# A depthwise 13x13 convolution by a two-output FIR scheme: three TensorE products in place of four, with the phases of its input stored apart

## The chip, the cores and the metric

The kernel runs on one core of a Trainium2 chip. Its engines work side by side, each through its own instruction queue: TensorE (PE: matmuls, with PEld its weight loads), VectorE (DVE), ScalarE (ACT), GpSimd (POOL) and SyncE (SP, which only issues DMAs). ACT and POOL issue DMAs too. The metric is the device time of one execution in microseconds (us), the median of several runs.

## What is computed

`x` is (T=4, B=8, 512, 512) fp32: 4 x 8 = 32 images of 512 x 512. Four layers follow one another, each a residual on a group norm (four groups, each of two neighbouring `b`, for each `t`):

```python
x = x + layer0(_gn(x), ...)       # spiking attention: lif(linear), q k^T v, linear, lif
x = x + layer1(_gn(x), w)         # depthwise 13x13, the same w for each channel
x = x + layer2(_gn(x), ...)       # 3x3, 8 to 8 channels, 8-bit quantised
x = x + layer3(_gn(x), ...)       # 3x3, 8 to 8 channels
...
def layer1(x, w):
    xp = jnp.pad(x, ((0, 0), (0, 0), (6, 6), (6, 6)), mode='reflect')
    return conv(xp, w, strides=(1, 1), padding='VALID', groups=8)
...
def _gn(v, G=4, eps=1e-5):        # over the two channels of a group and all pixels
    return (v - mean(v)) / sqrt(var(v) + eps)
```

`lif` makes each output of layer 0 a 0 or a 1 (a threshold on a running potential), so layer 0 adds spikes to `x`. Layer 2 quantises by `127 / max|gn(x)|`, so it needs the mean, the variance, the maximum and the minimum of layer 1's output before it can begin.

## The kernel before

**Layer 0** (L260 to L1112) goes over the 32 pairs (b, t) and for each over four tiles of 128 tokens. `unit` (L583 to L677) computes the q, k and v spikes by matmuls; in it GpSimd adds `h += twice` (L655, two adds of 128x512 in a row), whose result VectorE reads at L615. `settle` (L893) finishes the group norm of a later input; it raises to the power -1/2 on GpSimd (L184). `project_out` (L789 to L850) ends a tile: output matmuls (L803), ScalarE copies of the input into the tile `x1` (L819, two), the potential `v` (L825), two VectorE operations that add the spikes (`is_ge`, `add`, L827) with their statistics (L831), the reset of the potential (L833), then on GpSimd eight small copies that fill the reflected edges (L839), and one GpSimd DMA that writes the tile's 128 rows of 2096 bytes to DRAM (L844). There are 128 such tiles. In the tile a row is kept as four phases: column 4u + f of the padded row stands in phase f at place u (131 places).

**Layer 1** (class `Layer1`, L1190 to L1298) then goes over the four groups, in a group over two b, and over four t: 32 images. An image is loaded by two SP DMAs (`load_image`, L1168) into a tile `x` of 112 partitions (28 input rows x 4 phases) with 32 windows of 16 output rows x 131 places. `image_bands` (L1181, VectorE) makes four weight matrices of 112 x 64 (one for each shift z = 0..3 of u), with the norm's scale and the residual in them. The convolution along a row is then four products of shifted views, summed in PSUM; rows and phases are the contraction. In `image`, for each of four chunks of an image, eight matmuls (four z, two halves q, which write PSUM partitions 0 to 63 and 64 to 127) go into a bank `ps_conv1`:

```python
for z in range(SHIFTS):                       # L1220
    for q in range(2):
        ...
        nc.tensor.matmul(ps[q*M1:(q+1)*M1, :], lhsT=bt[:, z, :], rhs=xt[:, w0:w0+N_PS1, z:z+NV], ...)   # L1223
```

ScalarE evicts the bank with the norm's offset (L1230, 128x512), VectorE takes its statistics (L1232) and its maximum and minimum (L1238, two reductions). Eight DMAs store an image (L1245), four issued by ScalarE and four by GpSimd, 128 KB each. `ps_c` has four banks; `x` has three buffers, the output tile `xo` two. `next_norm` (L1270) makes the statistics of a finished group, among them two small matmuls (L165), and is placed after the first image of the next group.

**Layers 2 and 3** (from L1387) are written in an order set by hand and are not touched.

The order of instructions within each engine's queue in layers 0 and 1 is set when the kernel is built, by a planner with costs of its own, under the constraints of data and of `issue_after` (an instruction is placed no earlier than another). It is fixed in the program: on the chip each engine works through its queue in that order.

Of the kernel before, what the change touches and what calls it, by code (L numbers as in the profile page):

```python
# [35 lines left out]
F32 = mybir.dt.float32  # L36
# [25 lines left out]
X1_R, X1_U = N + 2 * R1, (D + 2 * R1) // PH  # L62
SHIFTS = 4
K1_P, M1 = W1_IN * PH, W1_OUT * PH
N_PS1 = 4
# [18 lines left out]
COLS = BN + ["L0_conv_gate_scale", "L0_conv_gate_shift"]  # L84

# [38 lines left out]
def network(ctx: ExitStack, tc: tile.TileContext, i: dict, out: bass.AP):  # L124
# [3 lines left out]
    x1d = [[tc.dram_tile([X1_R, PH * X1_U], F32, name=f"x1_{t}_{b}") for b in range(B)] for t in range(T)]  # L128
# [67 lines left out]
    mr1 = const.tile([P, G, T], F32, name="mr1")  # L196
# [3 lines left out]
    def norm1(g, psum):  # L200

        m, r = group_stats(
            st1[g].rearrange("p t b c k (h z) -> p t (b c k h) z", z=3), T, PAIR * NC * 4, None,
            avg, psum, f"x1_{g}", n_each=D // 4, share=0.5,
        )
        nc.vector.tensor_copy(r1[:, g, :], r)
        nc.vector.tensor_mul(mr1[:, g, :], m, r)
# [5 lines left out]
    with ExitStack() as s:  # L213
        head = layer0(
            s, tc, i, x_in, x1d, ident, block, avg, group_stats, group_steps, st1, norm1, band1d, r1,
            w_sum, shared,
# [18 lines left out]
    with ExitStack() as s:  # L235
        ps_1 = s.enter_context(pool("ps_2", space=PSUM))
        st2 = s.enter_context(pool("st2")).tile(
            [P, T, B, W1_N // 2 // N_PS1, 6], F32, name="st2"
        )
        layer1 = Layer1(  # L240
            s, tc, x1d, x2d, avg, group_steps, r1, mr1, st2, m2, r2, most, w_sum, head, ps_1, pool
# [18 lines left out]
def layer0(  # L260
    s, tc, i, x_in, x1d, ident, block, avg, group_stats, group_steps, st1, norm1, band1d, r1, w_sum, shared
# [28 lines left out]
    share = wpool.tile([3 * SQ, P], BF16, name="share")  # L290
# [61 lines left out]
    def phases(x):  # L352
        return x.rearrange("p (v g) -> p g v", g=PH)
# [97 lines left out]
    def prepare_out():  # L451
# [4 lines left out]
        nc.scalar.copy(scale.rearrange("p (g v) -> p g v", g=PH), phases(along_free(a_rows, 3)))  # L456
        wps = [scratch[:, 1 + k % 2, :] for k in range(NC)]

        def scaled(k):
            nc.scalar.mul(  # L460
                wps[k].rearrange("p (g v) -> p g v", g=PH), phases(wp_rows[k]),
                gate_scale[:, k : k + 1],
            )
# [21 lines left out]
        nc.scalar.copy(c_p.rearrange("p (g v) -> p g v", g=PH), phases(along_free(c_rows, 3)))  # L485
        shift = ps_mm.tile([P, D], F32, tag="mm", name="shift")
        for k in range(NC):
# [5 lines left out]
        nc.vector.tensor_mul(  # L493
            moved.rearrange("p (g v) -> p g v", g=PH), phases(shift),
            scale.rearrange("p (g v) -> p g v", g=PH),
        )
# [86 lines left out]
    def unit(kind, cc, n, got):  # L583
# [81 lines left out]
        if kind == "kv":  # L665
            op = nc.tensor.matmul(
                b, lhsT=share, rhs=c_step, start=False, stop=True, skip_group_check=True
# [121 lines left out]
    def project_out(so, c, xt, b, t):  # L789
# [3 lines left out]
        last = D + 2 * R1 - 1  # L793
# [18 lines left out]
        by_phase = phases(xt)  # L812
        halves = []
        for z in range(2):
            f, u = (2 * z + R1) % PH, (2 * z + R1) // PH
            two = slice(2 * z, 2 * z + 2)
            halves.append((two, x1[:, f : f + 2, u : u + NV]))
            with tc.issue_after(seeds[-1]):
                op = nc.scalar.copy(halves[z][1], by_phase[:, two, :])  # L819
# [6 lines left out]
        for z, (two, own) in enumerate(halves):  # L826
            nc.vector.scalar_tensor_tensor(  # L827
                own, v.rearrange("p (g v) -> p g v", g=PH)[:, two, :], 1.0, own,
                op0=ALU.is_ge, op1=ALU.add,
            )  # L830
# [3 lines left out]
        for f in range(PH):  # L834
            right = D + R1 + (f - R1 - D) % PH
            for first, end, mirror in ((f, R1, 2 * R1), (right, last + 1, 2 * (last - R1))):
                n = len(range(first, end, PH))
                u, fm, um = first // PH, (mirror - first) % PH, (mirror - first) // PH
                nc.gpsimd.tensor_copy(  # L839
                    x1[:, f, u : u + n], x1[:, fm, um - n + 1 : um + 1][:, ::-1]  # L840
                )
# [943 lines left out]
```

## Time and profile before

| what | value |
|---|---|
| median of 3 runs | 2706.03 us (2703.67 to 2710.02) |
| profiled execution | 2708.08 us |
| its span in the profile | 2706.3 us (1.8 us lie around it) |
| mean granted TensorE clock | 0.988 |
| PE busy over the span | 2601.4 us (96%) |
| DVE, ACT, POOL busy | 1938.4 (72%), 1239.0 (46%), 762.1 us (28%) |
| layer 0 | 0 to about 1854 us |
| layer 1, first to last matmul | 1853.6 to 2312.4 us |
| first image of layer 2's input made | 2322.6 us |

The span runs from the first to the last instruction that the profile holds. Each engine's busy time is the union of its instructions' times; a share of busy time says nothing by itself of what sets the end, since an average hides stages with different limits. A line of a group names the source line, engine, operation, output and inputs, shape and count; behind the first bar stand the busy time and the mean of one in ns, behind the second the idle time of the engine just before these instructions and what ended it. "<-issue" there means that the profile shows no semaphore that was waited for: the engine's own queue was occupied. An fp32 matmul appears as two records.

### The profile page before, as it was taken

Reading aid. Unit: us, or ns where it says so; the run is one execution under the profiler, and the core shown is the slowest. Engines: PE = TensorE matmul, PEld = TensorE weight load, DVE = VectorE, ACT = ScalarE, POOL = GpSimd, SP = SyncE. Lnnn points to the kernel's source line nnn. Section 1 sums busy time; section 2 is a strip of 40 time slices with the busy share of each in tenths; the row PEclk is TensorE's granted clock in tenths of the full one; section 3 lists DMA queues with packets and bytes.
Section 4 is the critical chain, followed back from the end, with each engine's and each line's share of the span. In section 5 each row is a group of like instructions: output and inputs, shape, how many; then the busy total and the mean of one; then the engine's idle time right before and its main releaser. Section 6 shows DMA issues by size and latency. Waiting matters only on the chain. (4 is left out here: it accounts for less than half of the span.)

```text
span 2706.3 us, 49605 instructions
## 1 busy us (share of the span) xinstructions
PE 2601.4 (96%) x18124; PEld 1502.4 (56%) x18124; DVE 1938.4 (72%) x4054; ACT 1239.0 (46%) x2093; POOL 762.1 (28%) x2040
## 2 busy tenths in 40 slices
PE   7899999999999999999999999998999999699999
PEld 4566666665666656666566566664333333344446
DVE  7877878779788787977877768756565556666550
ACT  1454554555545545455554554553212112566653
POOL 3322223223232222322312323223111111444440
PEclk9999999999999999999999999999999999889999
DMA  6553533434435344253443442446777778567755
GB/s 143 143 153 103 129 119 101 138 113 116 131 96 146 120 115 131 80 149 119 119 120 82 108 109 80 122 124 159 207 213 211 199 206 223 140 183 215 212 162 152
DMA packets 420664, 385.02 MB, mean 142 GB/s; under 512 B 22675, under 2 KB 339843, under 8 KB 420307
## 3 DMA queue, kind: packets, MB, share of 16 engines
q1 hardware_dynamic: 364659, 307.93, 43.8%
q0 software_dynamic: 16448, 51.27, 5.2%
q10 hardware_dynamic: 39312, 22.65, 3.0%
q8 instruction: 142, 2.33, 0.4%
q14 instruction: 103, 0.84, 0.1%
HBM read 278.09 MB, written 103.67 MB: 141 GB/s over the span
## 5 line engine op out<-in xcount | busy, mean ns | idle before, releaser
L1223 PE MATMUL ps_conv<-x,bt 112*64 112x512 f32 x2048 | 451.5, 596 | 5.2 <-DVE v_p L825 3.0
L839 POOL COPY x1s<-x1s 128x1 f32<-128x1 f32 x1000 | 194.2, 248 | 736.0 <-DVE x1s L827 703.8
L1223 PEld LDWEIGHTS ps_conv<-x,bt 112*64 112x64 f32 x2048 | 148.5, 136 | 297.5 <-issue 290.7
L803 PE MATMUL ps_out<-wp,so 128*128 128x512 f32 x1024 | 298.8, 435 | 5.9 <-ACT ps_out L800 4.1
L1230 ACT ACTIVATE xo<-ps_conv,off 128x512 f32<-128x512 f32 x128 | 87.9, 687 | 376.4 <-PE ps_conv L1223 314.8
L571 PE MATMUL ps_kv_b<-w_sums,x_sum 128*128 128x512 f32 x512 | 247.2, 605 | 10.1 <-DVE x_sum L940 7.7
L571 PE MATMUL ps_kv_a<-w_raw,x_raw 128*128 128x512 f32 x512 | 249.8, 606 | 7.3 <-ACT ps_kv_a L637 6.5
L803 PEld LDWEIGHTS ps_out<-wp,so 128*128 128x128 f32 x1024 | 191.1, 189 | 106.1 <-ACT ps_out L800 38.4
L1663 PE MATMUL ps_conv<-x,band_t 32*32 32x512 f32 x6144 | 231.2, 597 | 1.0 <-ACT o L1703 1.0
L655 POOL TENSOR_TENSOR h_kv<-h_kv,twice 128x512 f32<-128x512 f32 x96 | 126.4, 1339 | 340.3 <-ACT twice L652 339.8
L722 PE MATMUL ps_own<-table_own,v 128*128 128x256 bf16 x1536 | 191.8, 273 | 13.8 <-DMA table_own<-bias_parts 9.8
L722 PEld LDWEIGHTS <-v 128*128 128x128 fp8e4 x1536 | 148.2, 98 | 53.9 <-DMA table_own<-bias_parts 19.0
L1245 POOL DMA_DIRECT2D x<-xo x128 | 71.4, 564 | 343.8 <-ACT xo L1230 335.5
L1558 DVE SCALAR_TENSOR_TENSOR x<-ps_conv,inv,x 128x512 f32<-128x512 f32 x128 | 95.3, 750 | 101.7 <-PE ps_conv L1522 91.6
L758 ACT COPY ps_f<-ps_own 64x512 f32<-64x512 f32 x256 | 142.9, 558 | 37.6 <-issue 20.0
L571 PEld LDWEIGHTS ps_kv_b<-w_sums,x_sum 128*128 128x128 f32 x512 | 97.8, 193 | 112.1 <-issue 91.0
L1663 PEld LDWEIGHTS ps_conv<-x,band_t 32*32 32x32 f32 x6144 | 115.2, 103 | 72.9 <-issue 48.9
L819 ACT COPY x1s<-xr 128x256 f32<-128x256 f32 x250 | 151.9, 660 | 4.6 <-DVE h_p L833 2.3
L571 PEld LDWEIGHTS ps_kv_a<-w_raw,x_raw 128*128 128x128 f32 x512 | 95.1, 192 | 101.6 <-issue 82.6
L1185 DVE SCALAR_TENSOR_TENSOR bt<-band,r,eye 112x64 f32<-112x64 f32 x128 | 31.5, 367 | 166.1 <-PE ps_conv L1223 164.0
L1522 PE MATMUL ps_conv<-xq,band 64*64 64x512 bf16 x1536 | 127.2, 404 | 22.5 <-DVE x L1558 16.4
L799 ACT CAST so<-q 128x512 fp32r<-128x512 fp8e4 x128 | 78.8, 617 | 141.0 <-PE ps_out L803 137.0
(257 smaller groups left out, 5076.3 us busy)
## 6 DMA issues: line engine op xcount, KB each, us to landing
table_own<-bias_parts SPq DMA_DIRECT2D x128, 576.0 KB
x<-x SPq DMA_DIRECT2D x64, 917.0 KB
xq<-in_x SPq DMA_DIRECT2D x128, 256.0 KB
xr<-in_x SPq DMA_DIRECT2D x128, 256.0 KB
x<-x1s POOLq DMA_DIRECT2D x125, 262.0 KB, 2.7
out<-o SPq DMA_DIRECT2D x120, 256.0 KB
xs<-in_x SPq DMA_DIRECT2D x112, 256.0 KB
x<-x SPq DMA_DIRECT2D x128, 224.0 KB
```

Of the source, the lines that this page charges most:

```text
L571: mm = nc.tensor.matmul(ps, lhsT=x[:, kk, cc * P : (cc + 1) * P], rhs=w[:, :2, kk, :], start=start and kk == 0, stop=kk == 1, skip_group_c ...
L655: nc.gpsimd.tensor_add(h, c if t == 0 else h, twice[0])
L722: nc.tensor.matmul(out, lhsT=src[:, c, h].rearrange("p t e -> p (t e)"), rhs=table[:, z, u : u + HN], start=start and c == 0 and z == 0, s ...
L758: nc.scalar.copy(final[j][a][two * DH : (two + 1) * DH, :], rows[a * DH : (a + 1) * DH, :])
L803: nc.tensor.matmul(ps, lhsT=tokens[:, k, :], rhs=wpT[z][:, k, :], start=False, stop=k == NC - 1 and z == 1, skip_group_check=True,)
L819: op = nc.scalar.copy(halves[z][1], by_phase[:, two, :])
L839: nc.gpsimd.tensor_copy(x1[:, f, u : u + n], x1[:, fm, um - n + 1 : um + 1][:, ::-1])
L1223: mm = nc.tensor.matmul(ps[q * M1 : (q + 1) * M1, :], lhsT=bt[:, z, :], rhs=xt[:, w0 : w0 + N_PS1, z : z + NV], start=z == 0, stop=z == SH ...
L1230: nc.scalar.activation(xo[:, a, :], ps, AF.Identity, bias=off[:, t : t + 1])
L1522: mm = nc.tensor.matmul(ps[half, :], lhsT=w["band2"][halves[b], kind, dx, :], rhs=xq[halves[b], j % 2, dx : dx + PH, :], start=dx == 0 and ...
L1558: nc.vector.scalar_tensor_tensor(inner, ps, w["inv"], x, op0=ALU.mult, op1=ALU.add, accum_out=sums[:, 0, :] if summed else None,).ins
L1663: mm = nc.tensor.matmul(ps[c * QP : (c + 1) * QP, :], lhsT=band[g * QP : (g + 1) * QP, int(last), dx, :], rhs=src[:, dx : dx + PH, :], sta ...
```

## The change

Layer 1's sum along a row is done by a two-output scheme. Neighbouring outputs u = 2k and u = 2k + 1 are computed together from the even places E and the odd places O of the row. With the bands B0 to B3:

- shared = (B0 + B1) O[k] + (B2 + B3) O[k+1]
- odd output = shared + B1 (E[k+1] - O[k]) + B3 (E[k+2] - O[k+1])
- even output = shared + B0 (E[k] - O[k]) + B2 (E[k+1] - O[k+1])

That makes six products of 512 columns for two outputs of 512 in place of eight. In detail:

- `project_out` writes each row as eight phases (even u, then odd u, of each of the four); DRAM holds x1 as [row within a window and phase][window x 131]. A tile is written by nine GpSimd DMAs (L877 of the changed kernel) in place of one, its edges are filled by six copies (L874) in place of eight, and the spikes are added by three VectorE operations in place of two. Layout copies of layer 0's constants, done once, are doubled.
- `load_image` takes four SP DMAs with pieces of 4192 bytes in place of two with 524; `image_bands` has a fifth VectorE operation that makes two more matrices.
- `differences` (L1262) makes the tiles `d` (O - E, with the sign taken up in the bands): four subtractions of 112x1040 an image, three on GpSimd and one on VectorE.
- `image` works in two halves j: 4 shared products into a bank `ps_odd` (L1288), a ScalarE copy of it into a bank `ps_even` (L1305), 4 products into each: 12 a half, 24 an image in place of 32. `ps_c` has six banks.
- ScalarE's evictions (L1314) accumulate sums, and a `Square` over 128x1024 (L1320) accumulates the squares; VectorE's statistics of the output go. Maximum and minimum are taken over 1024 elements at once (L1329). `rest` of a half is emitted in the program after the next half's copy.
- Of an image's eight stores, ScalarE issues four and SP four (L1342).
- `next_norm` is placed after the second image of the next group and begins with five small VectorE operations (`gather`, L1382).

The diff, cut to these parts:

```diff
+def x1_rows(dst, row, n):
+
+    w, i = divmod(row, W1_OUT)
+    size = X1_W * X1_U
+    return bass.AP(
+        dst.tensor, dst.offset + i * PH * size + w * X1_U, [[PH * size, n], [size, PH], [1, X1_U]]
+    )
...
-    x1d = [[tc.dram_tile([X1_R, PH * X1_U], F32, name=f"x1_{t}_{b}") for b in range(B)] for t in range(T)]
+    x1d = [[tc.dram_tile([W1_OUT * PH, X1_W * X1_U], F32, name=f"x1_{t}_{b}") for b in range(B)] for t in range(T)]
...
-        halves = []
-        for z in range(2):
-            f, u = (2 * z + R1) % PH, (2 * z + R1) // PH
-            two = slice(2 * z, 2 * z + 2)
-            halves.append((two, x1[:, f : f + 2, u : u + NV]))
...
+        odd = bass.AP(
+            flat.tensor, flat.offset + X1_E + 1,
+            [flat.ap[0], [2 * X1_U - 1, 2], [X1_U, 2], [1, NV // 2]],
+        )
+        halves = [
+            (
+                xt.rearrange("p (k g) -> p g k", g=2 * PH)[:, 2 : 2 + PH],
+                x1[:, :, 1 : 1 + NV // 2],
+            ),
+            (xt.rearrange("p (k q f) -> p q f k", q=PH, f=2)[:, ::-3], odd),
+        ]
+        for x, own in halves:
             with tc.issue_after(seeds[-1]):
-                op = nc.scalar.copy(halves[z][1], by_phase[:, two, :])
+                op = nc.scalar.copy(own, x)
...
-        for z, (two, own) in enumerate(halves):
-            nc.vector.scalar_tensor_tensor(
-                own, v.rearrange("p (g v) -> p g v", g=PH)[:, two, :], 1.0, own,
-                op0=ALU.is_ge, op1=ALU.add,
-            )
+        for z, (_, own) in enumerate(halves):
+            cut = v[:, z * HN : (z + 1) * HN]
+            cut = cut.rearrange("p (f k) -> p f k", f=PH)
+            parts = [(cut, own)] if z == 0 else [(cut[:, 2 * e : 2 * e + 2], own[:, e]) for e in range(2)]
+            for on, to in parts:
+                nc.vector.scalar_tensor_tensor(to, on, 1.0, to, op0=ALU.is_ge, op1=ALU.add)
...
-        nc.gpsimd.dma_start(dst[at : at + P, :], flat)
...
+        for to, of in MIRRORED:
+            nc.gpsimd.tensor_copy(pair(flat, *to), pair(flat, *of))
+        cuts = [0, *range(W1_OUT - R1, P, W1_OUT), P]
+        for first, end in zip(cuts, cuts[1:]):
+            nc.gpsimd.dma_start(x1_rows(dst, R1 + c * P + first, end - first), x1[first:end])
...
-    row, n_half = PH * X1_U, W1_N // 2
-    for w0 in (0, n_half):
-        nc.sync.dma_start(
-            xt[:, w0 : w0 + n_half, :],
-            bass.AP(
-                src.tensor, src.offset + w0 * W1_OUT * row,
-                [[X1_U, K1_P], [W1_OUT * row, n_half], [1, X1_U]],
-            ),
-        )
-
-
-def image_bands(nc, bt, band, b, r, eye):
+    size, n_half = X1_W * X1_U, W1_N // 2
+    for j in range(N_1):
+        for first, end, w in ((0, M1, 0), (M1, K1_P, 1)):
+            nc.sync.dma_start(
+                xt[first:end].rearrange("p (q j w) u -> p j q (w u)", q=2, j=N_1)[:, j],
+                bass.AP(
+                    src.tensor, src.offset + first % M1 * size + (w + j * N_PS1) * X1_U,
+                    [[size, end - first], [n_half * X1_U, 2], [1, N_PS1 * X1_U]],
+                ),
+            )
...
+        scale, op = (nr, ALU.subtract) if z % 2 else (r, ALU.add)
         nc.vector.scalar_tensor_tensor(
-            split[0], band[:, :, b, z, :], r[:K1_P], split[1], op0=ALU.mult, op1=ALU.add
-        )
+            bt[:, z, :].rearrange("p (r o) -> p r o", o=PH), band[:, :, b, z, :], scale[:K1_P],
+            eye[:, z, :].rearrange("p (r o) -> p r o", o=PH), op0=ALU.mult, op1=op,
+        )
+    nc.vector.tensor_sub(bt[:, SHIFTS:, :], bt[:, 0:SHIFTS:2, :], bt[:, 1:SHIFTS:2, :])
...
+        self.dp = s.enter_context(pool("d1", 3))
...
+    def differences(self, xt, b, t):
+
+
+        nc, parts = self.nc, []
+        for j in range(N_1):
+            d = self.dp.tile([K1_P, 2, N_PS1, 2, X1_E - 1], F32, tag="d", name=f"d_{b}_{t}_{j}")
+            for q in range(2):
+                w0 = q * (W1_N // 2) + j * N_PS1
+                own = xt[:, w0 : w0 + N_PS1, :]
+                less = bass.AP(
+                    own.tensor, own.offset + X1_E,
+                    [own.ap[0], [X1_U, N_PS1], [1 - X1_E, 2], [1, X1_E - 1]],
+                )
+                own = bass.AP(
+                    own.tensor, own.offset,
+                    [own.ap[0], [X1_U, N_PS1], [X1_E, 2], [1, X1_E - 1]],
+                )
+                engine = nc.vector if (j, q) == (N_1 - 1, 1) else nc.gpsimd
+                engine.tensor_sub(d[:, q], own, less)
+            parts.append(d)
+        return parts
...
+        def products(ps, bands, src, start):
+
+            for z in range(2):
                 for q in range(2):
-                    w0 = q * n_half + a * N_PS1
                     mm = nc.tensor.matmul(
-                        ps[q * M1 : (q + 1) * M1, :],
-                        lhsT=bt[:, z, :],
-                        rhs=xt[:, w0 : w0 + N_PS1, z : z + NV],
-                        start=z == 0,
-                        stop=z == SHIFTS - 1,
+                        ps[q * M1 : (q + 1) * M1, :], lhsT=bt[:, bands[z], :],
+                        rhs=src(q)[:, :, z : z + n_v],
+                        start=start and z == 0, stop=z == 1, skip_group_check=True,
                     )
-            nc.scalar.activation(xo[:, a, :], ps, AF.Identity, bias=off[:, t : t + 1])
-            at = b % PAIR
-            nc.vector.bn_stats(self.st2[:, t, b, a, :], xo[:, a, :])
-            for end, op in ((hi, ALU.max), (lo, ALU.min)):
-                args = end[:, t, at, a : a + 1], xo[:, a, :], AX.X, op
-                if (b, t, a) == (B - 1, T - 1, n_half // N_PS1 - 1):
-                    self.last_ends.append(args)
-                else:
-                    op = nc.vector.tensor_reduce(*args)
-        if (b, t) == (0, 0):
-            self.started = mm.ins, op.ins
-        dst = self.x2d[t]
+            return mm.ins
+
+        for j in range(N_1):
+            d = parts[j]
+
+            def odd(q):
+                w0 = q * n_half + j * N_PS1
+                return xt[:, w0 : w0 + N_PS1, X1_E:]
+
+            shared = self.ps_c.tile([P, N_PS1 * n_v], F32, tag="conv", name="ps_odd")
+            products(shared, (SHIFTS, SHIFTS + 1), odd, True)
+            even = self.ps_c.tile([P, N_PS1 * n_v], F32, tag="conv", name="ps_even")
+            nc.scalar.copy(even, shared)
+            if self.due:
+                self.due.pop()()
+            self.started_mm = products(shared, (1, 3), lambda q: d[:, q, :, 1], False)
+
+            def rest(j=j, d=d, shared=shared, even=even):
+                products(even, (0, 2), lambda q: d[:, q, :, 0], False)
+                own = xo[:, j * N_PS1 : (j + 1) * N_PS1]
+                for par, ps in ((1, shared), (0, even)):
+                    nc.scalar.activation(
+                        own[:, :, :, par], ps.rearrange("p (w k) -> p w k", w=N_PS1), AF.Identity,
+                        bias=off[:, t : t + 1], accum_out=total[:, t, at, j, par : par + 1],
+                    )
+                flat = own.rearrange("p w k e -> p (w k e)")
+                square = self.op.tile([P, 2 * N_PS1 * n_v], F8, tag="square", name="square1", bufs=1)
+                nc.scalar.activation(
+                    square, flat, AF.Square, bias=self.m1[:, g, t : t + 1], scale=-1.0, saturate=False,
+                    accum_out=squares[:, t, at, j : j + 1],
+                )
+                for end, op in ((hi, ALU.max), (lo, ALU.min)):
+                    args = end[:, t, at, j : j + 1], flat, AX.X, op
+                    if (b, t, j) == (B - 1, T - 1, N_1 - 1):
+                        self.last_ends.append(args)
+                    else:
+                        self.started_op = nc.vector.tensor_reduce(*args).ins
+                if j == N_1 - 1:
+                    self.store(b, t, xo)
+
+            self.due.append(rest)
+        if (b, t) == (B - 1, T - 1):
...
+                engine = nc.sync if f % 2 else nc.scalar
...
+                if g > 0 and b % PAIR == 0 and t == 1:
...
+        def gather():
+            nc.vector.tensor_reduce(
+                mean, total.rearrange("p t b j e -> p t (b j) e"), AX.X, ALU.add
+            )
+            nc.vector.tensor_scalar_mul(mean, mean, 1.0 / n_each)
+            nc.vector.tensor_sub(m2, mean, self.m1[:, g, :].unsqueeze(2).to_broadcast(every))
+            nc.vector.tensor_mul(m2, m2, m2)
+            nc.vector.scalar_tensor_tensor(
+                m2, m2, -1.0 * n_each, squares, op0=ALU.mult, op1=ALU.add
+            )
+
+        gather()
```

## The prediction

> **What bounds the kernel now.** I read the page's engine shares, then busy time by windows, the groups of layer 1 with shapes kept apart, and the waits. Columns of the windows: stretch, length, busy time of PE, PEld, DVE, ACT, POOL, then clock, DMA share, GB/s.
>
> ```profile
> 0.00:1850.00 1850.00, 1787.90 (x7774) 1167.09 (x7775) 1463.47 (x3004) 930.36 (x1616) 512.38 (x1327) 0.99 0.44 118
> 1850.00:1900.00 50.00, 44.84 (x185) 15.26 (x185) 28.41 (x68) 6.75 (x10) 17.19 (x49) 0.93 0.96 223
> 2000.00:2100.00 100.00, 100.00 (x466) 34.02 (x466) 56.72 (x119) 19.94 (x29) 16.66 (x29) 1.00 0.76 209
> ```
>
> Layer 1 (1853.6 to 2312.4) is bound by TensorE alone: busy all 100 us of 100, full clock, DMA at 0.76, VectorE under 0.6, ScalarE at 0.2. Layer 0 is also TensorE's (1788 of 1850), GpSimd there at 28%.
>
> What TensorE's time is made of shows in two windows of 1.70 us (second figure in brackets counts matmul records):
>
> ```profile
> 1869.50:1871.20 1.70, 1.70 (x4) 0.55 (x5) 1.70 (x5) 0.45 (x1) 0.96 (x2) 1.00 1.25 252
> 2010.00:2011.70 1.70, 1.70 (x10) 0.57 (x8) 1.70 (x4) 0.69 (x1) 0.00 (x0) 1.00 1.17 239
> ```
>
> An fp32 matmul is two records. In the steady state the two column halves (q=0, q=1) run side by side: records start in pairs every 0.429 us, so two matmuls take u = 0.858 us. At 1869.5 several matmuls of one half stand in a row, and go one record per 0.43 us: a lone matmul takes a whole u. An image is 32 matmuls, 16 u = 13.73 us, and images do start 13.73 us apart (2006.86, 2020.59, 2034.34).
>
> The groups, and what ScalarE waits for, 1900 to 2300:
>
> ```profile
> L1223 PE MATMUL ps_conv<-x,bt 112*64 112x512 f32 x1816 | 395.7, 592 | 0.0
> L1230 ACT ACTIVATE xo<-ps_conv,off 128x512 f32<-128x512 f32 x114 | 78.4, 687 | 323.8 <-PE ps_conv L1223 285.8 <-issue 33.5 <-DMA x<-xo 4.4
> L1238 DVE TENSOR_REDUCE hi<-xo 128x1 f32<-128x512 f32 x115 | 76.9, 669 | 0.0
> ```
>
> And ScalarE's timeline where an image is stored:
>
> ```profile
> 2047.34 0.69 ACT L1230 ACTIVATE xo<-ps_conv,off 128x512 f32<-128x512 f32 x1 [2.76 <-PE ps_conv L1223]
> 2048.05 3.65 ACTq L1245 DMA_DIRECT2D x<-xo  x4
> 2052.04 0.69 ACT L1230 ACTIVATE xo<-ps_conv,off 128x512 f32<-128x512 f32 x1 [4.02 <-issue]
> ```
>
> Four DMA issues hold ScalarE 3.65 us here (2.77 to 4.41 over the images, 3.45 taken), and the next eviction starts 0.34 us later: "issue", no semaphore. Today four PSUM banks hide this.
>
> **What the Trainium skill says.** "TensorE: Matmul & The Clock Gate", "Part 3: Packing small matmuls": matmuls keep program order in start and end, only weight loads are pulled ahead. The windows above agree: a same-half run isn't overtaken. The same page, "Part 1: The HAM clock gate": the clock is judged in windows of 3413 ns and an idle one is followed by half clock. This trace agrees: clock changes lie on a 3.413 us grid, and each of twelve windows that fell to half clock followed one with TensorE streaming under 0.40 of it. "ScalarE: Activation LUTs", "What ACT_TABLE_LOAD costs": 280 ns + 0.833 ns per element with a pointer operand; 512 elements give 707 ns, the trace has 687. "DMA: Bandwidth & Descriptors", "Issuing engines are not separate DMA queues": moving a DMA to another engine saves sequencer time only; no row here contradicts it.
>
> **The change, part by part, per image.**
>
> *Products.* 24 matmuls for 32: 12 u = 10.30 us if all pair, -3.43. They would pair if issued as the source reads. The static order of the changed kernel's TensorE queue in the steady state differs: four x-products of half 0; then, behind the copy odd to even (`copy0`), odd0-d q0, even0 q0, odd1-x q0, odd0-d q1 and so on, the halves separated; then odd1-d and even1, paired. With strict order the 20 matmuls behind copy0 take 12 u = 10.30 us instead of 10 u. Lower bound 8.58.
>
> *The chain through ScalarE.* Its order is copy0, evict odd0, copy1, evict even0, square 0, evict odd1, evict even1, square 1, four store issues, then copy0 of the next image. TensorE's only work ahead of that copy is the next image's four x-products, 1.72 us. From even1's end to the next copy0's end: semaphore 0.10, evict 0.69, accumulator read and gap 0.09 (the layer 2 squares of 512 elements: 720 with a read of 187, mostly beneath), four issues 3.45 (the square, about 1.15 by the price above, and by layer 2's 1.24 for 1024 elements, lies beneath the first two, as issues were seen beside a running ACTIVATE), 0.12 gap, copy 0.57 (layer 0's PSUM copies: 570), semaphore 0.05: 5.07 us. If issues wait for the square: 6.2. If the four take 2.2 (4 x 0.54, the shortest): 3.8. So the period is 10.30 + 5.07 = 15.37 us against 13.73: +1.64, TensorE idle 3.35 us per image in one piece.
>
> *Clock.* A stall of 3.35 us laid on a 3.413 us grid leaves 2.1 us or more in one window in about three of four positions; the window after runs at half clock and costs about 1.5 us of its 1.7: 0.75 x 1.5 = +1.1. Bounds 0 and 1.7. Period 16.5, +2.75. Times 32: +88 us (no throttle: +52).
>
> *Differences.* Three `tensor_sub` of 1040 elements on GpSimd at 1.274 x 1040/512 = 2.6 us (from L655), 7.8 us; one on VectorE, about 1.4. VectorE loses four bn_stats (4 x 0.685) and reduces 1024 at a time (same elements, 5.2 us), bands +0.5: 7.8 us for 8.0. Neither reaches 13 us: nothing. Without that cover half 0's d-products would wait for GpSimd, up to 5 us.
>
> *Stores, loads.* Four store issues move from GpSimd to SP; queued behind them on SP is the load of the image three ahead, needed over a period later than its landing: nothing. Loads have 4192-byte pieces for 524; DMA doesn't bound layer 1 (0.76 busy while TensorE never waits): nothing.
>
> *Group boundaries, end, seam.* The five gather operations, and the group matmuls that TensorE meets ahead of the next x-products: 4.3 us for 2.0, three times, +7. End of the stage, evict, square and gather before the last norm: +2. Seam: GpSimd has the last five tiles' 45 issues, 25 us, ahead of image 0's differences, so its d-products start near 1871 instead of 1854; part is given back by image 1, which today waits for its load until 1874.13: +8 (0 to +17).
>
> *Layer 0.* Per tile, GpSimd issues nine DMAs for one and does six copies for eight:
>
> ```profile
> L844 POOL DMA_DIRECT2D x<-x1s x124 | 69.5, 561 | 39.4 <-POOL x1s L839 35.9 <-issue 2.9 <-DMA x<-x1s 0.6
> L655 POOL TENSOR_TENSOR h_kv<-h_kv,twice 128x512 f32<-128x512 f32 x96 | 126.4, 1339 | 340.3 <-ACT twice L652 339.8
> ```
>
> 8 x 0.56 - 2 x 0.25 = +4.0 us, 512 us in all; GpSimd goes from 28 to 55%, not the bound. But two of three pairs of the adds L655 start right behind such a DMA. From the first add's start to its reader on VectorE (L615) pass 5.1 to 6.2 us, the pair takes 2.56: 2.5 to 3.6 us of slack for 4.0 of delay, so 0.4 to 1.5, say 0.8, on 53 of the 80 pairs = 42 us late. TensorE has other tiles' work between; I take a third: +15. Bounds 0, and +60 (all of it, and the 16 settle steps by 1 us each). VectorE's third is_ge: 0.14 x 128 = 18 us on an engine at 79%, hidden; ScalarE's layout copies keep their count.
>
> *Sum.* The profiled execution's own time is 2708.1 (span 2706.3 and 1.8 around it): 2708 + 88 + 7 + 2 + 8 + 15 = 2828. It lies 2 above the runs' median of 2706: forecast 2826.
>
> **The rivals.**
> - No throttle, same chain: 2706 + 52 + 32 = 2790. For: a stall split by the few x-products keeps windows above 0.40. Against: windows at half clock in the trace after less idle than this.
> - Shorter chain (issues 2.2 us, period 14.2, or halves that pair after all, 13.7): 2706 + 0 to 15 + 32 = 2738 to 2753.
> - Layer 0 is hit in full: +60 for 15, 2871. For: TensorE there is at 97%, and every late spike step delays something. Against: its slack is of the same size as the delay.
> - Faster: the four issues don't hold copy0. Then even1's end to copy0's end is 5.07 - 3.45 = 1.62 us, less than the 1.72 us of x-products; TensorE never waits, and the period is between 10.3 (all pairs) and 12.0 (14 u): at 10.3, 2706 - 110 + 32 = 2628; at 12.0, 2683. It decides at a period of 13.73 less 1.0 (the +32 elsewhere): copy0 done within 2.4 us of even1's end. For: issues ran beside ACTIVATEs. Against: the timeline's 4.02 <-issue.
>
> **How the numbers follow.** A measurement here can tell 0.2% (5 us) from no change. Chances: forecast 0.38 (2800 to 2850), no throttle 0.20 (2760 to 2800), layer 0 in full 0.15 (2850 to 2890), shorter chain 0.13 (2720 to 2760), faster 0.14 (2620 to 2700, a little of it near no change). Slower 0.84, same 0.03, faster 0.13. Range 2730 to 2885: it leaves out the faster case and some 0.05 at each edge.
>
> **What would show it.** Right: images 15.4 to 16.5 us apart; TensorE busy 73 to 80% of layer 1 with a wait of about 3.3 us per image ended by ScalarE's copy; that copy after "issue"; clock near 0.9 in layer 1; in layer 0 GpSimd at 55% and VectorE waiting for its adds. Wrong: images under 13 us apart, or a copy that starts before the stores.

## The result, and the profile after

| | before | changed |
|---|---|---|
| median | 2706.19 us (4 runs) | 2843.55 us (4 runs, 2837.32 to 2845.87) |
| span of the profiled execution | 2706.3 us | 2840.0 us |
| mean granted clock | 0.988 | 0.962 |
| first matmul of layer 1 starts | 1853.56 | 1851.13 us |
| last eviction of layer 1's first four images starts | 1917.75 | 1968.35 us |
| last eviction of layer 1 starts | 2312.54 | 2436.34 us |
| from there to the end | 393.8 | 403.7 us |

The ratio is 1.0503 (1.0481 to 1.0524): slower by 137 us, forecast 2826, range 2730 to 2885. Each ratio here and below is to runs of the kernel before that were made beside it (medians 2705 to 2710 us).

First the windows of the changed kernel, in the columns of the windows before:

```profile
0.00:1850.00 1850.00, 1785.61 (x7771) 1164.77 (x7772) 1473.27 (x3136) 943.75 (x1620) 954.81 (x2040) 1.00 0.47 118
1875.00:1900.00 25.00, 3.43 (x6) 0.82 (x8) 0.00 (x0) 0.00 (x0) 18.95 (x29) 0.50 0.72 153
2100.00:2200.00 100.00, 79.52 (x284) 30.75 (x282) 60.14 (x83) 39.49 (x82) 43.75 (x19) 0.88 0.80 172
```

Layer 0 takes as long as before although GpSimd is busy 955 us for 512. Then TensorE waits for some 40 us; from 1875 to 1900 VectorE and ScalarE do nothing at all, and GpSimd is busy 19 us. In the second stretch of layer 1 TensorE is busy 80 of 100 us, where it was busy all the time before, at a clock of 0.88.

Some short names: x-products are the matmuls L1288 that read `x`, d-products those that read a tile `d`; odd0, even0, odd1 and even1 are the banks `ps_odd` and `ps_even` of an image's halves 0 and 1, so even1 is what ends an image. ScalarE's timeline there (start, length, instruction, then the idle time before it and what ended it):

```profile
2207.47 0.74 ACT L1314 ACTIVATE xo<-ps_even,off 128x512 f32<-128x512 f32 x1 [0.63 <-PE ps_even L1288]
...
2208.31 1.15 ACT L1320 ACTIVATE square<-xo,m 128x1024 fp8e4<-128x1024 f32 x1
2208.31 1.20 ACTq L1342 DMA_DIRECT2D x<-xo  x2
2209.36 0.19 ACT L1320 ACTIVATION_READ_ACCUMULATOR square<-xo,m 128x1 f32 x1
2209.56 2.10 ACTq L1342 DMA_DIRECT2D x<-xo  x2
2211.69 0.57 ACT L1305 COPY ps_even<-ps_odd 128x512 f32<-128x512 f32 x1 [2.15 <-issue]
```

and TensorE's over the same time:

```profile
2207.70 1.94 PE L1288 MATMUL ps_odd<-x,bt 112*64 112x512 f32 x8 [0.26 <-PE ps_even L1288]
2212.41 1.06 PE L1288 MATMUL ps_odd<-d,bt 112*64 112x512 f32 x2 [2.77 <-ACT ps_even L1305]
```

This is the chain of the prediction: the last eviction, the square with two issues beneath it, two issues alone, the copy; TensorE has its eight records of x-products (four matmuls) and then waits 2.77 us for the copy. Over the 22 images away from group boundaries the period, the time from one image's end to the next, is 16.37 us (16.5 forecast): 4.78 from even1's end to the next d-product (5.07), and 11.59 from there to the next even1's end. The latter is 10.0 us in the mean of six images that lie at full clock (9.8 to 10.3; forecast for broken pairs 10.3), and 11.8 in the mean of twelve that hold one window of 3.41 us at half clock and no other wait. Over all 22, half clock and a few short waits make 11.59 - 10.0 = 1.6 us an image (1.1 forecast for the clock).

The seam, on GpSimd's timeline and then TensorE's:

```profile
1869.34 7.83 POOL L877 DMA_DIRECT2D x<-x_last  x15
1878.33 0.51 POOL L877 DMA_DIRECT2D x<-x_last  x1 [1.16 <-DMA x<-x_last]
1882.52 1.14 POOL L877 DMA_DIRECT2D x<-x_last  x2 [3.68 <-DMA x<-x_last]
...
1889.42 4.69 POOL L877 DMA_DIRECT2D x<-x1s  x9
1894.03 6.61 POOL L1262 TENSOR_TENSOR d<-x 112x1040 f32<-112x1040 f32 x3
```

```profile
1896.39 1.97 PE L1288 MATMUL ps_odd<-d,bt 112*64 112x512 f32 x2 [41.60 <-POOL d L1262]
```

Image 0's x-products are done at 1855. Its differences stand on GpSimd behind 45 DMA issues of layer 0's last tiles, four of which wait for an earlier DMA to land, until 1894. TensorE waits 41.6 us.

### The profile page after: what moved, and what is told of

Same layout as the page of the kernel before. It is cut to its first block, busy times and chain, and to the rows that moved or that the text cites. A ratio compares the mean times of both kernels' runs of the same rounds, so it can differ in the third digit from the quotient of the medians.

```text
span 2840.0 us, 50906 instructions
## 1 busy us (share of the span) xinstructions
PE 2578.4 (91%) x17612; PEld 1516.2 (53%) x17612; DVE 2012.3 (71%) x4027; ACT 1381.8 (49%) x2419; POOL 1383.8 (49%) x2776
## 5 line engine op out<-in xcount | busy, mean ns | idle before, releaser
L877 POOL DMA_DIRECT2D x<-x1s x1125 | 598.9, 571 | 53.3 <-POOL x1s L874 30.4
L1262 POOL TENSOR_TENSOR d<-x 112x1040 f32<-112x1040 f32 x96 | 224.0, 2353 | 253.5 <-DMA x<-x 210.9
L874 POOL COPY x1s<-x1s 128x2 f32<-128x2 f32 x750 | 130.4, 245 | 418.2 <-DVE x1s L869 290.2
L1288 PE MATMUL ps_odd<-d,bt 112*64 112x512 f32 x512 | 226.3, 682 | 115.4 <-ACT ps_even L1305 68.7
L1329 DVE TENSOR_REDUCE hi<-xo 128x1 f32<-128x1024 f32 x63 | 76.6, 1216 | 202.6 <-ACT xo L1314 202.6
L1288 PE MATMUL ps_even<-d,bt 112*64 112x512 f32 x512 | 201.6, 624 | 0.0
L1288 PE MATMUL ps_odd<-x,bt 112*64 112x512 f32 x512 | 189.2, 646 | 9.4 <-DMA x<-x 7.7
L857 ACT COPY x1s<-xr 128x256 f32<-128x256 f32 x250 | 169.6, 680 | 19.1 <-DMA x<-x1s 7.7
L1288 PEld LDWEIGHTS ps_odd<-d,bt 112*64 112x64 f32 x512 | 59.9, 150 | 204.6 <-issue 130.0
L1779 PEld LDWEIGHTS ps_conv<-x,band_t 32*32 32x32 f32 x6144 | 117.6, 103 | 73.2 <-issue 48.3
```

Source lines behind the costliest of these rows:

```text
L857: op = nc.scalar.copy(own, x)
L874: nc.gpsimd.tensor_copy(pair(flat, *to), pair(flat, *of))
L877: nc.gpsimd.dma_start(x1_rows(dst, R1 + c * P + first, end - first), x1[first:end])
L1262: engine.tensor_sub(d[:, q], own, less)
L1288: mm = nc.tensor.matmul(ps[q * M1 : (q + 1) * M1, :], lhsT=bt[:, bands[z], :], rhs=src(q)[:, :, z : z + n_v], start=start and z == 0, stop ...
L1779: mm = nc.tensor.matmul(ps[c * QP : (c + 1) * QP, :], lhsT=band[g * QP : (g + 1) * QP, int(last), dx, :], rhs=src[:, dx : dx + PH, :], sta ...
```

## The experiments

The theory: (1) ScalarE's store issues between an image's last eviction and the next image's copy set layer 1's period; (2) broken pairs cost 0.43 us each; (3) at the seam the differences wait for GpSimd's queue. The rivals: loads, differences or DMA set the period; or layer 0 lost the time. All edits below are to the changed kernel, if not said otherwise; none changes what is computed. The planner sets the order of the queues anew for each edit, so an edit can move more than its own lines; where that decides the reading (runs 6 and 10), it is said.

**1. Stores off ScalarE** (SP issues all eight):

```diff
-                engine = nc.sync if f % 2 else nc.scalar
+                engine = nc.sync
```

> All eight stores of an image are issued by SP, none by ScalarE; nothing else is edited. Theory (ScalarE's four store issues stand between an image's last eviction and the next image's copy, and TensorE has only 1.72 us of work over that time): from even1's end to the copy's end 1.6 us in place of 5.1, no stall, a steady period of 12.0 us in place of 15.85 (the pairs stay broken), so 29 x 3.85 = 112 us less: about 2732. Rival A (the stall is the wait for loads or for the differences, and the copy only stands last): period stays above 15, 2820 to 2850. Rival B (SP now issues eight stores ahead of each load and becomes the queue that is late): 2760 to 2830, with TensorE or GpSimd waiting for DMA x.

Measured: 2823.34 us, ratio to before 1.0415 (1.039 to 1.044). Only 20 us less: the period is 16.10 us in the mean, but now every other image takes 12.5 us and those between 18 to 21. The ranges of rivals A and B both hold this time, and the trace shows what they share, a load that comes late: SP needs 5.4 us for an image's eight stores before it issues the next load, and in the chain of waits from 2200 to 2260 these stores and the load make up 58% of the time.

**2. Stores behind the copy** (ScalarE's four stay, placed later):

```diff
-            nc.scalar.copy(even, shared)
+            self.copied = nc.scalar.copy(even, shared).ins
...
-                    self.store(b, t, xo)
+                    with self.tc.issue_after(self.copied):
+                        self.store(b, t, xo)
```

> ScalarE still issues four stores per image, but they are held until the copy of the next image has been issued; the amount of work on each engine is unchanged. Theory (place, not amount): the same as with the stores on SP, period 12.0, about 2732. Rival A (loads or differences late): 2820 to 2850. Rival C (ScalarE's amount of issue time counts, wherever it stands): the copy of half 1 is then late by the same 3 us, 2830 to 2850.

Measured: 2799.92 us, 1.0342 (1.0306 to 1.0377). With the same work on ScalarE 44 us go, so its place counts; but 112 were expected, and the time lies in none of the three ranges. From even1's end to the next d-product it is now 3.11 us for 4.78, at least 2.7. The expectation had the copy done 1.6 us after even1's end, and overlooked that the copy needs the x-products, which only end 1.72 us after it: with this order of TensorE's about 1.0 us of the wait stays. And the rest of the image, 9.8 us in every other image (so the pairs are broken as before), is 12.7 to 17.4 in those between. What ends that second wait stands on SP's and GpSimd's timelines of this run:

```profile
2237.66 2.76 SPq L1343 DMA_DIRECT2D x<-xo  x4
2241.90 2.55 SPq L1206 DMA_DIRECT2D x<-x  x4
```

```profile
2249.91 2.22 POOL L1262 TENSOR_TENSOR d<-x 112x1040 f32<-112x1040 f32 x1 [6.65 <-DMA x<-x]
2254.71 5.45 POOL L1262 TENSOR_TENSOR d<-x 112x1040 f32<-112x1040 f32 x2 [2.57 <-DMA x<-x]
```

The load of image n + 2 stands on SP behind image n's stores, and its halves are there 8 and 13 us after its issue begins; then come the differences. In the changed kernel itself the times are nearly the same (issue at 2215.44, differences at 2223.34 and 2227.84, the last eviction of the image before at 2224.71): the load arrives about when it is needed. Behind the wait for ScalarE stood a second one of nearly its length.

**3. Products in program order.** Each product is held behind the one before it:

```diff
-                    mm = nc.tensor.matmul(
+                    with self.tc.issue_after(self.before) if self.before else ExitStack():
+                        mm = nc.tensor.matmul(
...
+                    self.before = mm.ins
```

> Each TensorE product of layer 1 is held behind the one before it in the program, so that the halves q stay adjacent, and the x-products of an image stand ahead of the last even products of the image before; ScalarE's copy then comes ahead of evict even1 and the stores by data alone. Theory (a broken pair costs 0.43 us, and the copy no longer waits for the stores): 12 u = 10.3 us a period unless another engine is slower: 29 x (15.85 - 10.3) = 161 us less, about 2682. Rival D (then DMA binds: 2.93 MB an image at 215 to 250 GB/s is 11.7 to 13.6 us): 2722 to 2778. Rival E (pairs broken or not are worth nothing): no better than the version with stores off ScalarE, about 2732 or more.

Measured: 2926.94 us, 1.0803 (1.0768 to 1.0838): worse by 83 us, period 19.9. TensorE's timeline:

```profile
2119.99 1.91 PE L1290 MATMUL ps_even<-d,bt 112*64 112x512 f32 x8
2122.04 2.64 PE L1290 MATMUL ps_odd<-d,bt 112*64 112x512 f32 x8
2130.75 3.68 PE L1290 MATMUL ps_odd<-x,bt 112*64 112x512 f32 x8 [6.06 <-DMA x<-x]
```

The pairs are whole (elsewhere in this timeline eight records follow each other every 1.7 us), but now the x-products of image n + 1 stand in front of the last products of image n. So they wait for a load that SP issues behind the stores of image n - 1; those stores wait for image n - 1's last eviction, and that for the x-products of image n. The loop closes in 20 us. TensorE waits for loads 147 us in all. None of the expectations held; the second limit found in run 2 explains it, and run 7 tests that.

**4. Layer 0's last tiles by SP:**

```diff
-            nc.gpsimd.dma_start(x1_rows(...), x1[first:end])
+            (nc.sync if late else nc.gpsimd).dma_start(x1_rows(...), x1[first:end])
```

> The row DMAs of layer 0's last eight tiles (b = 7, t = 2 and 3) are issued by SP in place of GpSimd; layer 1 is unchanged. Theory (image 0's differences wait in GpSimd's queue behind 45 DMA issues, until 1894): they start at about 1865 to 1870, 20 to 30 us less: 2813 to 2823. Rival (the start is set by when the rows of the last tiles have landed and memory is free, or SP's loads move back by as much): 0 to 8 us less, 2835 to 2843.

Measured: 2854.67 us, 1.0536 (1.0511 to 1.0561), 11 us more, beyond both ranges. GpSimd is free 30 us before, but the differences begin no earlier (1894.64), after a wait that the landing of a last tile's row DMA ends; and the loads of images 1 and 2 come later, behind SP's issues. So it isn't GpSimd's queue alone that holds the differences: they wait for these DMAs, whichever queue issues them. Why they need them (the expectation of run 8 takes it for memory used again) no trace shows.

**5. The kernel before with nine DMAs per tile** (edit to the kernel before):

```diff
-        nc.gpsimd.dma_start(dst[at : at + P, :], flat)
+        cuts = [0, *range(W1_OUT - R1, P, W1_OUT), P]
+        for first, end in zip(cuts, cuts[1:]):
+            nc.gpsimd.dma_start(dst[at + first : at + end, :], flat[first:end])
```

> The kernel before, with only layer 0's write of a tile cut into nine GpSimd DMAs of whole rows in place of one (same layout, all else as before): layer 0's cost of the change alone. Theory now (the changed kernel's layer 0 ends 2.5 us earlier than before's, so 4 us more of GpSimd per tile are hidden, and only layer 1's differences, which this kernel has not, ever wait for them): 2704 to 2712, GpSimd busy over 50% of layer 0. The prediction's term: +15 us, 2721. Rival (the copies for the eight phases or fewer edge copies hid a loss): 2720 to 2770.

Measured: 2726.17 us, 1.0075 (1.0057 to 1.0093), +21, in the rival's range. Layer 1's first matmul comes 6.5 us later (1860.09), and by the end of its third image it is 20 us, since image 1's load waits. So the cut costs little inside layer 0, and most of it where layer 1 takes over.

**6. GpSimd in place of SP for four stores**, as in the kernel before:

```diff
-                engine = nc.sync if f % 2 else nc.scalar
+                engine = nc.gpsimd if f % 2 else nc.scalar
```

> The changed kernel, with the four stores that it moved to SP issued by GpSimd as in the kernel before; ScalarE keeps its four. Theory (two limits stand close together: ScalarE's chain of even1, evict, stores, copy; and behind it on SP the loop store, load, landing, which the versions without ScalarE's stall ran into): the chain alone stays, so a little is gained where loads were late: period 15 to 15.6, and layer 2's first loads no longer wait behind stores: 2815 to 2835. Rival (SP's stores are free): 2840 to 2848. Rival (GpSimd's differences come behind the stores and are late): 2850 to 2880.

Measured: 2845.39 us, 1.0513 (1.0494 to 1.0532), as the changed kernel, with a period of 16.70. But the reason is another one. The planner set other orders here: ScalarE copies for the next image ahead of this image's last eviction and its stores, so that TensorE doesn't wait for that copy. It waits for something else (ScalarE's, GpSimd's, VectorE's and TensorE's timelines):

```profile
2221.17 0.57 ACT L1305 COPY ps_even<-ps_odd 128x512 f32<-128x512 f32 x1
2223.76 1.20 ACTq L1342 DMA_DIRECT2D x<-xo  x2
```

```profile
2227.46 4.37 POOL L1262 TENSOR_TENSOR d<-x 112x1040 f32<-112x1040 f32 x2
```

```profile
2227.93 4.07 DVE L1224 TENSOR_TENSOR bt<-bt 112x128 f32<-112x128 f32 x1
```

```profile
2232.09 1.08 PE L1288 MATMUL ps_odd<-x,bt 112*64 112x512 f32 x1 [4.03 <-issue]
```

VectorE's subtraction of two bands takes 4.07 us (0.27 at its shortest) and ends 0.17 us after GpSimd's two differences; the x-products of the next image, which need these bands, start 0.09 us later. In 25 images of this run TensorE sits idle for 4 us or more until then. Run 7 comes back to this. So run 6 doesn't tell what freeing SP gains while ScalarE's chain stands; no run does. One thing it does show: from layer 1's last eviction to the end it is 391.2 us for 403.7: layer 2's first loads no longer stand behind SP's stores. The changed kernel and the runs with stores on SP (1 to 4 and 8) have 399 to 404 there, those with none there (6, 7, 9 to 12) 391 to 396.

**7. Program order and GpSimd's stores** (edits 3 and 6):

> Both: TensorE's products in program order, and the four stores by GpSimd in place of SP, so that SP only loads. Theory (in the version with program order alone, the next load waited on SP behind the stores of the image in work, the stores for its last eviction, and that in TensorE's order for the x-products that need the load: a loop of 20.3 us; without stores on SP the loop is open): period 10.3 to 11.5, about 2670 to 2715. Rival D (DMA binds at 215 to 250 GB/s): period 11.7 to 13.6, 2720 to 2775. Rival (the loop is one of landing times, not of the queue): above 2850.

Measured: 2760.41 us, 1.0205 (1.019 to 1.0221), 83 less than the changed kernel and 167 less than program order alone. So the loop over SP is real. The period is 13.46, though, not 10.3 to 11.5, in the middle of rival D's range. What ends TensorE's wait is the same as in run 6. GpSimd's timeline, then VectorE's:

```profile
2216.12 4.38 POOL L1263 TENSOR_TENSOR d<-x 112x1040 f32<-112x1040 f32 x2
```

```profile
2216.57 4.08 DVE L1224 TENSOR_TENSOR bt<-bt 112x128 f32<-112x128 f32 x1
2220.57 1.23 DVE L1263 TENSOR_TENSOR d<-x 112x1040 f32<-112x1040 f32 x1
```

VectorE's subtraction of two bands takes 4.08 us and ends 0.15 us after GpSimd's two differences do; TensorE's next x-products begin at 2220.75, after 2.10 us of waiting. "SBUF — State Buffer" in the Trainium skill, "SBUF: two separate sides", says that a VectorE operation with two SBUF inputs and a GpSimd operation that reads SBUF exclude each other: the one that starts first has a shared port pair for its whole instruction. The trace agrees, and shows the wait to last over two GpSimd instructions in a row.

**8. Layer 0's last tiles on three queues:**

```diff
+            engine = (nc.gpsimd, nc.scalar, nc.sync)[k % 3] if late else nc.gpsimd
```

> The row DMAs of layer 0's last eight tiles go in turn to GpSimd, ScalarE and SP; layer 1 is unchanged. With SP alone image 0's differences began no earlier (1897): their buffer takes memory of tiles whose DMAs were still being issued there. Theory (the time is that of issuing some 45 DMAs through one queue, whichever it is): three queues need a third, the differences begin at about 1872 to 1880, 15 to 25 us less: 2818 to 2829. Rival (landing, or loads on SP that come later by as much): 2838 to 2850.

Measured: 2815.51 us, 1.0413 (1.0385 to 1.0441), 28 less, as the theory has it or a little better. The differences begin at 1879 for 1894, and image 0 ends 16.5 us sooner; 18 of the 28 us lie in the first four images. With run 4 this says that the issuing of these DMAs through one queue sets the time, not which queue it is.

**9. All differences on VectorE** (with edits 3 and 6):

```diff
-                engine = nc.vector if (j, q) == (N_1 - 1, 1) else nc.gpsimd
+                engine = nc.vector
```

> As the version with program order and GpSimd's stores, with all four differences of an image on VectorE in place of three on GpSimd. There VectorE's small subtraction of the bands took 4.1 us in place of 0.28 whenever GpSimd ran two differences beside it, and TensorE's next x-products waited for it. Theory (GpSimd's and VectorE's two-input operations from SBUF exclude each other, and this holds the period at 13.5): the bands take 0.28 us again, VectorE has 4 x 1.23 + 4 x 1.21 + 1.4 = 11.2 us an image, period 11.2 to 11.8, so 2690 to 2715. Rival (DMA binds, busy 0.87 at 200 GB/s): unchanged, 2750 to 2765.

Measured: 2705.16 us, 0.9998 (0.9981 to 1.0015): 55 less than run 7, no different from before. Rival D falls, as the windows of run 7 and of this run show:

```profile
2000.00:2100.00 100.00, 80.05 (x324) 28.93 (x326) 85.95 (x92) 42.45 (x89) 57.31 (x47) 0.90 0.82 193
2000.00:2100.00 100.00, 88.70 (x388) 28.03 (x386) 84.03 (x128) 52.07 (x112) 18.34 (x33) 0.95 0.97 239
```

DMA moves 239 GB/s where run 7 had 193. The subtraction of the bands never takes over 0.29 us in this run. (The edit also replaces GpSimd's 2.2 us a difference by VectorE's 1.2, so that the exclusion is the limit of run 7 rests on run 7's timelines, not on this time alone.) Most images now take 10.4 to 11.4 us, six of 22 take 14 to 17. At the seam VectorE has nothing else to do, and yet image 0's differences begin only at 1887, when a row DMA of a last tile has landed:

```profile
1887.13 5.85 DVE L1263 TENSOR_TENSOR d<-x 112x1040 f32<-112x1040 f32 x5 [23.30 <-DMA x<-x1s]
```

**10. The planner's order again** (edits 2, 6 and 9):

> As the run with all differences on VectorE and GpSimd's stores, but TensorE's products in the planner's order (halves separated) and the stores held behind the next image's copy, so that neither the chain over ScalarE, nor SP's loop, nor the shared port holds it: what the broken pairs cost by themselves. Theory: 12 u and a little, period 12.0 to 12.6, 2710 to 2740. Rival (broken pairs cost nothing, since another engine sets the period): within 6 us of the run in program order.

Measured: 2701.50 us, 0.9982 (0.9967 to 0.9996). The time is the rival's, but it doesn't answer the question: the planner left the pairs nearly whole here, and most images take 10.5 to 11.1 us as in run 9. What broken pairs cost is shown only inside single images: 9.8 us at the least for 20 matmuls in the changed kernel, against 1.73 us for each four, 8.6 for 20, in run 12.

**11. With the seam on three queues** (edits 3, 6, 8 and 9):

> The run with all differences on VectorE, program order and GpSimd's stores, and layer 0's last eight tiles written by three queues in turn: if the four causes found add up, the seam's 28 us come off again: 2660 to 2690, faster than the kernel before. Rival (image 0's differences, now on VectorE, no longer wait for GpSimd's issues, so that nothing is left to gain there): the same as without it, within 8 us.

Measured: 2706.20 us, 0.9994 (0.9984 to 1.0004), as without. Image 0's last eviction starts at 1893.2 for 1902.1 in run 9, but image 3's at 1949.3 for 1951.1, and the last one's at the same time. So what is gained at the seam is lost again in images 1 to 3; the four gains don't add up.

**12. All stores by GpSimd** (edits 3 and 9, and `engine = nc.gpsimd`):

> The run with program order and all differences on VectorE, with all eight stores of an image issued by GpSimd, which is 82% idle there in layer 1, and none by ScalarE or SP. In that run most images take 10.4 to 11.4 us, but one in three or four takes 14 to 17, when ScalarE's copy stands behind its own store issues. Theory (the same ScalarE wait as in the changed kernel, now met only at times): all steady images take 10.4 to 11.2, 28 x 1.2 = 34 us less: 2665 to 2680, faster than the kernel before by 1 to 1.5%. Rival (those long images are DMA falling behind, busy 0.95 at 228 GB/s, and the issue waits are its sign): 2695 to 2710.

Measured: 2649.63 us, 0.9794 (0.978 to 0.9807): 2.1% faster than the kernel before, 194 us less than the changed one, and 15 us below the theory's range. Its windows:

```profile
2000.00:2100.00 100.00, 94.39 (x430) 30.29 (x426) 95.41 (x159) 56.99 (x128) 42.00 (x76) 0.98 1.00 269
2100.00:2200.00 100.00, 96.47 (x432) 31.31 (x434) 91.29 (x138) 52.43 (x117) 40.78 (x72) 0.97 0.98 260
```

Of the 22 images 20 take 10.3 to 10.6 us, TensorE's 10.3 for 12 pairs and a little, where the kernel before takes 13.73. So three products for four do give three quarters of the time, once no copy stands behind store issues, no load behind stores, and VectorE makes all differences. DMA moves 269 GB/s: 209 was no limit.

## Why the prediction was right, and where its terms were off

The direction and the mechanism of layer 1 were right: the time is 18 us above the forecast, within the range, and the chain over ScalarE is there piece by piece. Most of its signs came: images 16.4 us apart, TensorE busy 78 to 81% with a wait that ScalarE's copy ends, the clock at 0.88 to 0.95, GpSimd at 52% in layer 0. That the sum came so close is in part luck, since its terms miss both ways. By terms, in the two profiled executions (+133.7 us, forecast 120):

| term | forecast | measured |
|---|---|---|
| layer 0, to layer 1's first matmul | +15 | -2.4 |
| images 0 to 3 (seam 8, chain 4 x 2.75) | +19 | +53.0 |
| images 4 to 31 (chain 77, boundaries 7) | +84 | +73.2 |
| after layer 1's last eviction | +2 | +9.9 |

- **Chain, clock, broken pairs**: within 1% of the period, with small misses that cancel. The four issues take 3.0 us (3.45), the stall is 4.78 - 1.72 = 3.06 us (3.35), the 20 matmuls behind the copy 10.0 (10.3), half clock and short waits 1.6 (1.1).
- **Layer 0**: taken as a third of the bound, +15; the changed kernel shows nothing. VectorE does wait for GpSimd's adds there, 28.6 us in all, but layer 0 isn't longer for it. Run 5 shows what the cut does by itself: 6.5 us at layer 0's end. That the other edits of layer 0 give these back isn't shown.
- **Seam**: the mis-sized term, +8 for 53.0 - 11 = +42. The step let 45 issues of 0.56 us run from about 1846 to 1871. They run from 1865 to 1894: GpSimd first has the tiles' copies and earlier issues, and the 45 take 29 us, not 25, since four wait for an earlier DMA to land. It also took the place in GpSimd's queue for the cause, where the differences wait for the DMAs themselves (runs 4 and 9). Of the "part given back" little came: image 1 takes 10.9 us, image 3 12.5. Another wait of 17 us lies in image 2, around the small matmuls that make layer 2's weights (ahead of 1950 us), which cost about 4 us over six images before; no run tried it alone, but the last section shows what fills part of it.
- **Stores and loads on SP, "nothing"**: wrong twice. The load lands 8 to 13 us after its issue, so that the "period later" is used up, which the ScalarE wait hid (runs 1, 2, 3 and 7); and at layer 1's end layer 2's loads stand behind the stores, some 10 us (run 6).
- **Differences, "nothing"**: true of the steady images here, but priced as if both engines were alone. VectorE's difference takes 2.67 us in the mean (1.4 forecast, 1.23 beside no GpSimd operation in run 7); with the other two limits gone this was the bound (runs 6 and 7). The forecast's 7.8 us of VectorE work doesn't come out of its own figures either (5.2 + 0.5 + 1.4 = 7.1); nothing hung on it.
- **The rival on the faster side** had the right place (issues ahead of the copy) and the wrong price: moving them alone gains 20 to 44 us of 137, since the next limits, 15 to 16 us (SP, runs 1 and 2) and 13.5 (VectorE and GpSimd, run 7), lay within 3 us of the 16.4.

The boundary was forecast at 4.3 us for 2.0. A boundary image and the next take 35.9 us together, for 29.5 before; 2 x 2.63 of that is the chain's, so the boundary itself costs about 1.1 us more than before, not 2.3.

## What to carry to other kernels

When an engine that was 100% busy loses a quarter of its work, list every loop through another queue that takes more than the new period: here a copy behind DMA issues on ScalarE, loads behind stores on SP, and VectorE shut out by GpSimd, each 13 to 16 us an image against 10.3. Removing the first shows only the second. And where a planner sets the queues, look in the trace of each experiment whether the order is still the one that it is meant to test (run 6). A DMA issue is work of the engine that issues it (0.54 to 2.2 us each on ScalarE in the changed kernel): put stores on a queue with nothing urgent behind them, and give loads a queue of their own.

## What the runs showed that was not expected

- The exclusion of VectorE and GpSimd lasts over back-to-back GpSimd instructions (run 7), and also meets small one-input operations. In image 2 of the changed kernel three VectorE operations on 128x4 take 2.2 us each beside GpSimd's three differences, two of them with one input; a copy of that size takes 0.17 us where GpSimd is idle. Here each gets in behind one GpSimd operation. They stand ahead of the small matmuls for layer 2's weights, and make over 6 us of the 17 that TensorE waits there:

```profile
1937.50 6.50 POOL L1262 TENSOR_TENSOR d<-x 112x1040 f32<-112x1040 f32 x3
1937.55 2.17 DVE L234 COPY r<-grstd_x 128x4 f32<-128x4 f32 x1 [1.16 <-POOL grstd_x L212]
1939.64 2.24 DVE L235 TENSOR_SCALAR nr<-grstd_x 128x4 f32<-128x4 f32 x1
1941.79 2.23 DVE L237 TENSOR_TENSOR mr<-gmean_x,grstd_x 128x4 f32<-128x4 f32 x1
```

- The share of busy DMA time is no measure of what is left: 209 GB/s stood at 0.76 before, 172 at 0.80 in the changed kernel, 269 at 1.00 in run 12.
